# Product and composed tables loaded through GpSimd's queue, deeper buffers for the last group, longer pauses between two interleaved groups

## The chip, the cores and the metric

The kernel is one program on one core of a Trainium2 chip. The metric is device time in microseconds, the median of several executions. One profiled execution comes with it; it gives busy times, waits and a timeline of each engine. The engines are PE (TensorE, matmuls), DVE (VectorE), ACT (ScalarE), POOL (GpSimd) and SP (SyncE, which here only issues transfers, DMAs).

## What is computed

The input x is [16, 32, 128, 128] in float32. Four residual layers follow one another, each of them x = x + f(GroupNorm(x)):

- layer 0: a recurrent convolution with gates, run over the columns of a skewed image;
- layer 1: a 3x3 "adder" convolution on 8-bit values, which sums absolute differences in place of products;
- layer 2: a Hartley transform of which 32 x 32 modes are mixed between channels;
- layer 3: five edge operators, each normalised by its own mean and deviation, then a small U-net (seven 3x3 convolutions, pooling, three transposed convolutions), whose output multiplies the layer's input.

```python
# layer 1, for each of 32 outputs
out[n, f] = -sum(abs(patch(qx) - qw[f]))
# layer 2
xm = dht2d(x)[:, :, :32, :32]
z = einsum('bixy,ioxy->boxy', xm, yeven) + einsum('bixy,ioxy->boxy', flip(xm), yodd)
out = dht2d(embed(z)) / (H * W)
# layer 3
y = concat([norm(edge_k(x)) for k in range(5)]); y = conv1(y); y = maxpool2(y) ...
return x * conv7(deconv3(...))
```

## The kernel before

**Stages.** `stage0` (line 101) does layer 0 in about 870 us. `rest` (441) does layers 1 to 3. Layer 1 runs image by image in `Differences.run` (627). DVE (line 705, tile d_dve) and ACT (line 702, tile d_act) make the differences, 128 x 8192 elements in fp16 at a time, and PE adds them up by matmuls with a selection matrix (line 592). Layers 2 and 3 go in four groups of four images. As soon as the four images of a group have left layer 1, its later layers are woven between the instructions of layer 1 for the next images. That is the work of the class `Weave`: the background work is a Python generator that yields estimated durations, negative numbers as pauses, and marks for things that must be complete; `later(us, step)` puts a step off by so many estimated microseconds, and `advance` (384) puts background work into gaps of the planned schedule. `keep_order` (419) then pins the order of instructions on each engine for this whole stretch, which lasts from about 890 to 5989 us. I call it the front.

**The drain.** When layer 1 is over, the rest of the third group (number 2) and the whole of the last group (number 3) remain. `drain` (403) takes steps of the two generators in turn, always from the one that is behind, and so puts the two groups' instructions side by side; there is no pinned order there. The last group is a copy of the object `After` with pools on the other side of SBUF and an accumulator pool of its own. The drain takes from 5989 us to the end.

**One group**, in order:

1. `forward` (974): loads rows of the image (tile xh, four buffers, 992), centres them (DVE, 1014), transforms along both axes with matmuls (1061, 1076, 1031). The 32 x 32 modes come out of PSUM by a DVE copy into xm (1035, two buffers) and are stored to DRAM (1041). `modes` (1105) reads them back in another arrangement into xs and xw (1114, xw has two buffers), and DVE adds the flipped copy (1121, 1128). `weights` (1134) loads the mixing matrices, 1 MB each (tile mix, 1136, three buffers).
2. `mixing` (1139): 512 matmuls (1149), results stored to z_d. It yields pauses of 5 us at line 1159.
3. `back` (1176): reads z (1198) and the residual rows xr (1191, four buffers), transforms back (1212, 1257), adds (1235), stores x3 (1241). The images of layer 3's input go in frames of 16 rows with a margin, tile xp, a ring of two (`frames`, 1280; load 1299, normalise on ACT 1301, zeroed edges by POOL 1308).
4. `statistics` (1320): the means and deviations of the edge operators come from products of the image with shifted copies of itself (PE, 1345), multiplied with five tables gm of 210 KB each (DVE, 1405 and 1406, tile es_w). Three gm buffers are filled at line 1333, tables 3 and 4 at line 1412, once a buffer is free.
5. `first_layers` (1445): the edge operators and conv1 are composed into one set of weights wf (DVE, 1471 and 1473) from ten tables v of 720 KB each (1458, three buffers). `conv1` (1603) applies them (PE 1617, 1633, 1661), reading the frames again.
6. `small_layers` (1485) and `Composed.round` (838, matmuls 849 and 874) do the U-net's inside, `last` (1717) the last convolution, the multiplication with the layer's input (tile xr, loaded at 1731 into two buffers, each a quarter of the rows of the four images, in four DMAs; multiplied at 1752, evicted from PSUM at 1789) and the store (1768).

All these loads and stores are issued by SP, one after the other in one queue. If an issue has to wait for a buffer or for data, everything after it in the program waits behind it.

Of the kernel before, what the change touches and what calls it, by code (L numbers as in the profile page):

```python
# [19 lines left out]
M1 = 32  # L20
# [279 lines left out]
class Weave:  # L300
# [10 lines left out]
    def __init__(self, work):  # L311
        self.work, self.pending = work, None
        self.pe = self.dve = self.act = self.now = self.base = 0.0
        self.until = self.ready = 0.0
        self.draining = self.alone = False
        self.finished, self.count, self.put_off, self.for_act, self.ends = -1, 0, [], [], {}

    def later(self, us, step):
        self.count += 1
        v = self.base + us, self.count, step  # L320
        self.put_off.append(v)
        return v
# [36 lines left out]
    def step(self):  # L359

        v = self.pending or next(self.work, None)
        self.pending, wait, us = None, 0.0, 0.0
        if v is None:
            return None
        if v is SUMMED:
            wait = self.lag()
        elif isinstance(v, tuple) and v[0] == "done":
            late = v[1] in self.put_off
            self.done(v[1])
            end = self.ends[v[1][1]]  # L370
            wait = 2.0 * late if self.draining else end - self.now + 0.3
        elif isinstance(v, tuple):
            if v[1] > self.finished:
                self.pending = v
                return None
        elif v < 0:
            wait = -v
        else:
            us = v
        if wait > 0:  # L380
            self.until = self.now + wait
        return us
# [20 lines left out]
def drain(*weaves):  # L403

    live = list(weaves)
    for w in live:
        w.draining = True
    while live:
        w = min(live, key=lambda w: w.now)
        us = w.step()  # L410
        w.now = max(w.now + (us or 0.0), w.until)
        w.due(float("inf") if us is None else w.now)
        if us is None:
            live.remove(w)
            for w in live:
                w.alone = True

# [23 lines left out]
def rest(nc, tc, cst, sel16, bias, m1, r1, a, d, out):  # L441


    with ExitStack() as ctx:
# [13 lines left out]
        end.side, end.ps = "right", ctx.enter_context(tc.tile_pool(name="c_ps", bufs=4, space=PSUM))  # L458
        end.spare = bg
        end.weave = Weave(end.work([NG - 1]))  # L460
        end.weave.now = end.weave.base = weave.now
# [441 lines left out]
class After:  # L903


    def __init__(self, nc, tc, side, sm, ps, cst, bias, a, d, stat, out):
        self.nc, self.tc, self.side, self.ps, self.cst, self.bias = nc, tc, side, ps, cst, bias
        self.a, self.d, self.stat, self.out = a, d, stat, out
        self.spare, self.banks = None, 0
        store = [d["up"][i] for i in range(3)]  # L910
        self.up5 = Composed(nc, sm, a, "deconv1", "conv5", bias[:, 7:8], bias[:, 4:5], store[0])
# [62 lines left out]
    def forward(self, g):  # L974

        nc, tc, cst, d, weave = self.nc, self.tc, self.cst, self.d, self.weave
        x2, xm_d, z_d = d["x2"], d["xm"], d["z"]
        with self.pool("t_m") as mp:
            mr = mp.tile([128, 2, 4, C], F32, name="mr")
# [5 lines left out]
            with self.pool("t_t") as tp, ExitStack() as rows:  # L985
                xp = rows.enter_context(self.pool("t_x", 4))

# [6 lines left out]

                xh = [load(n) for n in range(4)]
                mv = tp.tile([128, 4, 2], F32, name="mv2")
# [29 lines left out]
                def second(n):  # L1026
# [6 lines left out]
                    def out():  # L1033
                        xm = tp.tile([128, 4, M1], F32, name="xm", bufs=2)
                        nc.vector.tensor_copy(xm.rearrange("p q k -> p (q k)"), p[:, :128])
# [44 lines left out]
                for n in range(10):  # L1080
                    if n < 7:
                        centred(n + 1)
                    if n < 8:
                        yield first(n)
                        if n + 4 < 8:
                            xh.append(load(n + 4))
                    if 1 <= n < 9:
# [8 lines left out]
                rows.close()  # L1096
                wp = rows.enter_context(self.pool("t_w", 3))
                wt = [self.weights(wp, i) for i in range(3)]
                yield -36.0
# [5 lines left out]
    def modes(self, g, b, pool, xs, steps):  # L1105

        nc, weave, xm_d = self.nc, self.weave, self.d["xm"]
        xw = pool.tile([128, 16, 32], F32, name="xw", bufs=2)
        first = xm_d.offset + (4 * g + b) * 32768
# [29 lines left out]
    def mixing(self, g, xs, wp, wt):  # L1139
# [5 lines left out]
        for ky in range(M1):  # L1145
# [12 lines left out]
            yield 1.0  # L1158
            if ky % 4 == 3 and 8 < ky < M1 - 1:
                yield -5.0  # L1160
# [15 lines left out]
    def back(self, g, load):  # L1176


        nc, tc, cst, d, weave = self.nc, self.tc, self.cst, self.d, self.weave
        x2, x3, z_d = d["x2"], d["x3"], d["z"]  # L1180

        with self.pool("t_z") as zp_, self.pool("t_r", 4) as rp:

# [12 lines left out]
            for blk in range(4):  # L1196
# [3 lines left out]
                )  # L1200
            for n in range(4):
                residual(n)
# [27 lines left out]
            def take_out(n, pf):  # L1230
# [9 lines left out]
                def store():  # L1240
                    nc.sync.dma_start(rows(n)(x3), xr[n])
                    ready[n + 4] = weave.later(6.0, lambda: reload(n + 4)) if n < 12 else None

                ready[n + 4] = weave.later(4.0, store)

# [24 lines left out]
            take_out(*previous)  # L1270
            weave.later(7.0, lambda: [load(ch, half) for ch in range(2) for half in range(2)])
            mv = zp_.tile([128, 1, 2], F32, name="mv3")
# [7 lines left out]
    def frames(self, g, pool):  # L1280
# [4 lines left out]
        nc, x3, weave = self.nc, self.d["x3"], self.weave  # L1285
        ring = [pool.tile([128, 20, W + 4], F32, name=f"xp{i}") for i in range(2)]
        for t in ring:
            nc.vector.memset(t[:, :, 0], 0.0)
            nc.vector.memset(t[:, :, W + 3], 0.0)

        def parts(ch, half):

            lo, hi = max(16 * ch - 2 + 10 * half, 0), min(16 * ch + 8 + 10 * half, H)
            off = lo - (16 * ch - 2)
            return ring[ch % 2], lo, hi, ring[ch % 2][:, off : off + hi - lo, 2 : W + 2]

# [19 lines left out]

        chunk = lambda ch: ring[ch % 2]
        return load, normalise, chunk

    def statistics(self, g, pool, frames, sides, out, tables):  # L1320
# [8 lines left out]
        load, normalise, chunk = frames  # L1329
        ready = {(n // 2, n % 2): normalise(n // 2, n % 2, 0.5 + 4.0 * n) for n in range(4)}  # L1330
        gm = [pool.tile([128, GRAM], F32, name="gm", bufs=3) for _ in range(3)]
        for k in range(3):
            nc.sync.dma_start(gm[k], self.a["gram"][:, k])
        f = pool.tile([128, 24], F32, name="es_f")
# [19 lines left out]
        for ch in range(H // 16):  # L1354
            xp = chunk(ch)
            yield ("done", ready[ch, 0])
            for l in range(2, 18):
# [28 lines left out]
                def following(ch=ch, half=half):  # L1386
                    load((ch + 2) % 8, half)
                    if ch + 2 < H // 16:
                        ready[ch + 2, half] = normalise(ch + 2, half, 18.0)

                ready[ch + 2, half] = weave.later(2.0, following)
            yield -1.0
# [9 lines left out]
        for k in range(5):  # L1402
            for blk in range(4):
# [4 lines left out]
                if blk % 2:  # L1408
                    yield -1.0
            if k < 2:  # L1410
                gm.append(pool.tile([128, GRAM], F32, name="gm", bufs=3))
                nc.sync.dma_start(gm[k + 3], self.a["gram"][:, k + 3])
        yield -2.0
# [31 lines left out]
    def first_layers(self, g, fp, frames, y2):  # L1445
# [4 lines left out]
        b1 = fp.tile([128, 4], F32, name="b1")  # L1450
        with self.pool("e_v", 3) as pool:
            v = []

            def table():

                k, half = len(v) // 2, len(v) % 2
                v.append(pool.tile([128, 45, 32], F32, name="v"))
                nc.sync.dma_start(
                    v[-1].rearrange("p t o -> p (t o)"), self.d["fold"][k, :, 1440 * half : 1440 * half + 1440]
                )  # L1460

            with self.pool("e_s") as es:
                yield from self.statistics(g, es, frames, sides, ops, lambda: [table() for _ in range(3)])
            yield -0.5
# [138 lines left out]
    def conv1(self, g, pool, frames, y1, sides, wf, b1):  # L1603
# [9 lines left out]
        load, normalise, chunk = frames  # L1613
        ready = {(n // 2, n % 2): normalise(n // 2, n % 2, 4.0 + 3.0 * n) for n in range(4)}
        p = self.acc()
# [33 lines left out]
        for ch in range(H // R):  # L1649
# [38 lines left out]
            yield SUMMED  # L1688
            if ch + 2 < H // R:
                for half in range(2):  # L1690
                    load(ch + 2, half)
                    ready[ch + 2, half] = normalise(ch + 2, half, 26.0 + 4.0 * half)
            out = []
# [23 lines left out]
    def last(self, g):  # L1717

        nc, tc, cst, weave = self.nc, self.tc, self.cst, self.weave
        with self.pool("l_y") as yp, self.pool("l_x", 2) as xp:  # L1720
            y6 = self.y6
# [11 lines left out]

            xr = [load(0), load(1)]

# [30 lines left out]
            def store(x, unit):  # L1766
                for j in range(4):
                    nc.sync.dma_start(at(self.out, unit, j), x[32 * j : 32 * j + 32])
                following[unit] = weave.later(10.0, lambda: reload(unit)) if unit < 2 else None

            def reload(unit):
                xr[unit] = load(unit + 2)
                following[unit] = None
# [5 lines left out]
            for unit in range(4):  # L1779
                complete(unit - 2)  # L1780
                x = xr[unit % 2]
                for pr in range(2):
# [186 lines left out]
```

## Time and profile before

| | before |
|---|---|
| median of 7 runs | 7224.34 us (7214.95 to 7239.58) |
| profiled execution | 7239.58 us, of which the span of the profile is 7237.6 us |
| PE busy | 5640.6 us, 78% |
| DVE busy | 5846.7 us, 81% |
| ACT busy | 5501.1 us, 76% |
| POOL busy | 52.1 us, 31 instructions |
| DMA, mean rate over the span | 100 GB/s |

The profiled execution happens to be the slowest of the seven, 15.2 us above the median. The page's second part divides the span into 40 equal slices of 181 us, with one digit for the busy tenths of each engine. From slice 6 to slice 33 DVE and ACT stand at 8 or 9, which is the front; from slice 34 on PE is the busiest. A list of waits gives for every engine the line that waited, the thing it waited for, the sum in us, the number of waits and the longest. A timeline line gives the start, the duration, engine, line and tiles, and in square brackets how long the engine had been idle and who released it.

### The profile page before, as it was taken

The page shows a single profiled execution, that of the slowest core. Times are in us where ns is not written, and L with a number is a line of the kernel's source. Part 1 is how long each engine was busy: PE and PEld are TensorE (multiplying, and loading weights), DVE is VectorE, ACT ScalarE, POOL GpSimd, SP SyncE. Part 2 cuts the span into 40 slices and gives each one's busy share as a digit, 9 for nine tenths or more (in the row PEclk, how much of TensorE's full clock was granted, in tenths as well). Part 3 has the DMA queues.
Part 4 walks back from the last instruction along what each step waited for, and adds up shares of the span by engine and source line. Part 5 has one row for each costly group of instructions (what it writes and reads, how often), then busy time and mean ns, then how long its engine had stood idle before and what let it go on. Part 6 is the DMA issues. An engine that isn't in the chain of part 4 may idle for free. (4 is left out here: it accounts for less than half of the span.)

```text
span 7237.6 us, 271421 instructions
## 1 busy us (share of the span) xinstructions
PE 5640.6 (78%) x127740; PEld 3009.0 (42%) x127740; DVE 5846.7 (81%) x7095; ACT 5501.1 (76%) x3100; POOL 52.1 (1%) x31
## 2 busy tenths in 40 slices
PE   4878567777777776999777786999776775797896
PEld 3666333333434342333334342333332443544564
DVE  7787699999989988999999998999998994234324
ACT  2555399999999988999999998999998991121222
POOL 0000000000000000000000000000000000000000
PEclk9899799999989898999888997999888997798897
DMA  8664211111132432221343343121243245352324
GB/s 312 227 203 150 78 65 57 51 58 51 43 111 83 141 101 70 63 74 44 77 123 105 111 121 96 61 66 50 64 112 99 79 128 140 95 157 83 86 59 104
DMA packets 374319, 722.57 MB, mean 100 GB/s; under 512 B 50896, under 2 KB 219856, under 8 KB 362320
## 3 DMA queue, kind: packets, MB, share of 16 engines
q1 hardware_dynamic: 372768, 704.58, 32.1%
q8 instruction: 999, 16.37, 1.0%
q14 instruction: 120, 0.98, 0.0%
q10 hardware_dynamic: 432, 0.64, 0.0%
HBM read 507.28 MB, written 164.32 MB: 93 GB/s over the span
## 5 line engine op out<-in xcount | busy, mean ns | idle before, releaser
L702 ACT ACTIVATE d_act<-q,neg 128x8192 f16<-128x8192 f16 (+1 forms) x631 | 4464.1, 7145 | 243.3 <-PE acc L592 193.6
L705 DVE TENSOR_SCALAR d_dve<-q,qw 128x8192 f16<-128x8192 f16 (+1 forms) x1673 | 3858.5, 2361 | 194.8 <-PE acc L592 152.6
L592 PE MATMUL acc<-d_dve,sel 128*32 128x512 f16 x26768 | 1868.5, 402 | 551.9 <-DVE d_dve L705 504.4
L592 PEld LDWEIGHTS <-sel 128*32 128x32 f16 x36864 | 1026.1, 100 | 2219.9 <-issue 1566.7
L1661 PE MATMUL acc<-xp,wf 32*32 32x512 f32 x25600 | 1033.1, 621 | 28.1 <-issue 22.8
L592 PE MATMUL acc<-d_act,sel 128*32 128x512 f16 x10096 | 730.1, 411 | 359.9 <-ACT d_act L702 348.9
L1661 PEld LDWEIGHTS acc<-xp,wf 32*32 32x32 f32 x25600 | 425.0, 104 | 396.0 <-issue 311.2
L622 PE MATMUL acc<-q,zero 128*32 128x512 f16 x7248 | 520.3, 399 | 0.0
L207 PE MATMUL pg<-h,wb 64*64 64x20 f32 (+15 forms) x4096 | 402.9, 323 | 96.4 <-DVE h L256 54.7
L1600 ACT ACTIVATE y<-pooled,b 32x128 f32<-32x128 f32 x488 | 195.0, 400 | 372.4 <-DVE pooled L1586 365.9
L849 PE MATMUL acc<-y,u_conv 32*32 32x256 f32 (+1 forms) x9728 | 353.3, 462 | 80.8 <-issue 51.8
L1305 ACT ACTIVATE xp<-xp,shift,stats 128x1280 f32<-128x1280 f32 (+1 forms) x128 | 182.9, 1434 | 277.2 <-DMA xp<-x_d 264.0
L244 ACT ACTIVATE gt<-pg,bias 128x20 f32<-128x20 f32 (+15 forms) x1024 | 315.7, 375 | 77.5 <-PE pg L207 70.7
L207 PE MATMUL pg<-e,wb 64*64 64x20 f32 (+15 forms) x4096 | 358.8, 319 | 16.9 <-DVE e L260 4.5
L207 PEld LDWEIGHTS pg<-h,wb 64*64 64x64 f32 x4096 | 249.9, 156 | 132.7 <-DVE h L256 82.4
L622 PEld LDWEIGHTS <-zero 128*32 128x32 f16 x7248 | 218.0, 101 | 201.0 <-issue 43.0
L207 PE MATMUL pg<-xn,wb 64*64 64x28 f32 (+61 forms) x4096 | 287.0, 305 | 9.6 <-ACT gt L244 3.0
L207 PEld LDWEIGHTS pg<-e,wb 64*64 64x64 f32 x4096 | 254.4, 157 | 95.6 <-DVE e L260 67.4
L1345 PE MATMUL acc<-xp 32*64 32x204 f32 (+3 forms) x8576 | 243.1, 343 | 35.8 <-ACT xp L1311 25.7
L255 ACT ACTIVATE th<-c 128x20 f32<-128x20 f32 (+15 forms) x256 | 81.3, 320 | 238.7 <-DVE c L253 237.3
L849 PEld LDWEIGHTS acc<-y,u_conv 32*32 32x32 f32 x9728 | 171.1, 110 | 190.5 <-issue 126.7
L1789 DVE TENSOR_SCALAR s<-acc,l_ms,l_one 128x512 f32<-128x512 f32 x128 | 101.9, 821 | 164.6 <-PE acc L849 164.6
(212 smaller groups left out, 4263.9 us busy)
## 6 DMA issues: line engine op xcount, KB each, us to landing
xr<-x_d SPq DMA_DIRECT2D x192, 512.0 KB
xp<-x_d SPq DMA_DIRECT2D x112, 640.0 KB
q<-q_d SPq DMA_DIRECT2D x32, 2145.0 KB
x_d<-xr SPq DMA_DIRECT2D x128, 512.0 KB
x_in<-in_x_dram SPq DMA_DIRECT2D x16, 2048.0 KB
res<-in_x_dram SPq DMA_DIRECT2D x64, 512.0 KB
xn<-in_xs_dram SPq DMA_DIRECT2D x64, 512.0 KB
xn<-xn SPq DMA_DIRECT2D x128, 256.0 KB
```

The source lines that it names most:

```text
L207: nc.tensor.matmul(bank[c][q][64 * pair : 64 * pair + 64, :, :width], wb[half, 4 * kind + KIND[q]].rearrange("p b o -> p (b o)"), v[half], ...
L244: nc.scalar.activation(gt[:, q, :, :n], bank[c][q][:, :, :n], AF.Tanh if q == G else AF.Sigmoid, bias=bias[:, KIND[q] : KIND[q] + 1],)
L592: self.nc.tensor.matmul(acc[k][32 * j : 32 * j + 32, :], self.sel16[:, i // 9, :], d[:, row : row + 4, c : c + W], start=first, stop=last,)
L622: self.nc.tensor.matmul(acc[k][32 * j : 32 * j + 32, :], self.zero, q[:, :4, :W], start=False, stop=False)
L702: nc.scalar.activation(dst, src, AF.Relu, bias=self.neg[:, i : i + 1])
L705: nc.vector.tensor_scalar(dst, src, self.qw[:, i : i + 1], 0.0, ALU.subtract, ALU.max)
L849: nc.tensor.matmul(acc[blk][32 * j : 32 * j + 32, o : o + rows * n], t[part, 4 * par + tap, :], src[part, top : top + rows, left : left + ...
L1305: nc.scalar.activation(v, v, AF.Identity, bias=self.shift3, scale=self.stats3[:, 1])
L1345: nc.tensor.matmul(gram[blk][j : j + width, at : at + n], xp[part, l, 2 + j : 2 + j + width], xp[part, rows, j : j + width + 4], start=sta ...
L1600: nc.scalar.activation(d, s, AF.Identity, bias=bj)
L1661: nc.tensor.matmul(acc[blk][32 * j : 32 * j + 32, :], tap_of("all", tap)[rows], xp[rows, 4 * j + kh : 4 * j + kh + 4, kw : kw + W], start= ...
L1789: nc.vector.tensor_scalar(s.rearrange("p r w b -> p b r w"), acc[blk].rearrange("p (b r w) -> p b r w", b=2, w=64), istd[:, blk : blk + 1] ...
```

## The change

1. The loads of the tables gm (lines 1333 and 1412) and v (1458) are issued by GpSimd instead of SP: 15 loads for each group, 60 in all.
2. Buffer numbers are taken from a dictionary. In the front xm gets three buffers instead of two; the other numbers stay (xh 4, xw 2, mix 3, xr 4, frames 2, gm 3, v 3, xr of the last layer 2). For the last group, which runs in the drain, all are raised: xh 8, xm 8, xw 4, mix 6, xr 8, frames 4, gm 5, v 6, xr of the last layer 4. Loads ahead and conditions for reloads follow these numbers.
3. While two groups are drained side by side, pauses and `later` times are multiplied by 1.5; when one is left, by 1.
4. The pauses of 5 us in `mixing` are left out while draining.

```diff
     def later(self, us, step):
-        v = self.base + us, self.count, step
+        v = self.base + us * self.stretch, self.count, step
...
         elif v < 0:
-            wait = -v
+            wait = -v * self.stretch
...
     for w in live:
-        w.draining = True
+        w.draining, w.stretch = True, 1.5
...
             for w in live:
-                w.alone = True
+                w.alone, w.stretch = True, 1.0
...
+        end.buffers = {"t_x": 8, "xm": 8, "xw": 4, "t_w": 6, "t_r": 8, "frames": 4, "gm": 5, "e_v": 6, "l_x": 4}
         end.weave = Weave(end.work([NG - 1]))
...
+        self.buffers = {"t_x": 4, "xm": 3, "xw": 2, "t_w": 3, "t_r": 4, "frames": 2, "gm": 3, "e_v": 3, "l_x": 2}
...
-                        xm = tp.tile([128, 4, M1], F32, name="xm", bufs=2)
+                        xm = tp.tile([128, 4, M1], F32, name="xm", bufs=self.buffers["xm"])
...
-            if ky % 4 == 3 and 8 < ky < M1 - 1:
+            if ky % 4 == 3 and 8 < ky < M1 - 1 and not weave.draining:
                 yield -5.0
...
-        gm = [pool.tile([128, GRAM], F32, name="gm", bufs=3) for _ in range(3)]
-        for k in range(3):
-            nc.sync.dma_start(gm[k], self.a["gram"][:, k])
+        gm = [pool.tile([128, GRAM], F32, name="gm", bufs=tables_ahead) for _ in range(tables_ahead)]
+        for k in range(tables_ahead):
+            nc.gpsimd.dma_start(gm[k], self.a["gram"][:, k])
...
-                nc.sync.dma_start(gm[k + 3], self.a["gram"][:, k + 3])
+                nc.gpsimd.dma_start(gm[-1], self.a["gram"][:, len(gm) - 1])
...
-        with self.pool("e_v", 3) as pool:
+        with self.pool("e_v", self.buffers["e_v"]) as pool:
...
-                nc.sync.dma_start(
+                nc.gpsimd.dma_start(
                     v[-1].rearrange("p t o -> p (t o)"), self.d["fold"][k, :, 1440 * half : 1440 * half + 1440]
                 )
...
-        with self.pool("l_y") as yp, self.pool("l_x", 2) as xp:
+        with self.pool("l_y") as yp, self.pool("l_x", self.buffers["l_x"]) as xp:
...
-            xr = [load(0), load(1)]
+            xr = [load(unit) for unit in range(ahead)]
```

## The prediction

> **What bounds the kernel now.** I read the page's first and second parts, then the waits of DVE and ACT in the front, then the timelines around the longest of them, then the drain by windows. The page first:
>
> ```profile
> PE 5640.6 (78%) x127740; PEld 3009.0 (42%) x127740; DVE 5846.7 (81%) x7095; ACT 5501.1 (76%) x3100; POOL 52.1 (1%) x31
> DVE  7787699999989988999999998999998994234324
> ACT  2555399999999988999999998999998991121222
> ```
>
> The shares of the whole span mislead. From slice 6 to 33 (890 to 5989 us) DVE and ACT are both full; a hole there in both engines is lost time, and work on POOL or SP costs nothing while it is off their path. From slice 34 on neither is full, and PE carries the drain. The waits of DVE in the front:
>
> ```profile
> DVE d_dve L705 <- PE acc L592: 152.6, 94, 14.6
> DVE es_w L1405 <- DMA gm<-in_gram_dram: 40.3, 2, 24.6
> ...
> DVE xm L1035 <- DMA xm_d<-xm: 34.6, 3, 25.0
> DVE xw L1121 <- DMA xw<-xm_d: 13.7, 4, 5.3
> DVE wf L1473 <- DMA v<-fold_d: 10.9, 4, 7.2
> ```
>
> Three of them hang on tables or buffers that the change touches. The first hole for gm, on SP's queue, DVE and ACT:
>
> ```profile
> 2711.07 0.33 SPq L1412 DMA_DIRECT2D gm<-in_gram_dram  x1
> 2711.44 0.55 SPq L559 DMA_DIRECT2D q<-q_d  x1
> 2718.22 0.33 SPq L1412 DMA_DIRECT2D gm<-in_gram_dram  x1
> ```
>
> ```profile
> 2755.60 0.60 DVE L1405 TENSOR_TENSOR es_w<-acc,gm 128x420 f32<-128x420 f32 x1 [24.60 <-DMA gm<-in_gram_dram]
> ```
>
> ```profile
> 2767.13 14.14 ACT L702 ACTIVATE d_act<-q,neg 128x8192 f16<-128x8192 f16 x2 [17.02 <-PE acc L592]
> 2783.49 7.13 ACT L702 ACTIVATE d_act<-q,neg 128x8192 f16<-128x8192 f16 x1 [2.23 <-PE acc L592]
> ```
>
> The last table was issued in time (2718) but came at 2755, behind the 2145 KB load of q that SP had issued just before. DVE stood 24.6 us, and ACT 17.0 + 2.2 soon after, since PE's accumulators came late. The second hole (4410) is DVE 15.7, ACT 11.4 + 1.8. The drain (PE busy by windows: 112 of 240 us from 6000, then 344 of 360, 132 of 180, 231 of 260, 132 of 197) is open at its start, in its middle and at its end. At the end:
>
> ```profile
> 7187.45 1.41 DVE L1752 SCALAR_TENSOR_TENSOR xr<-xr,l_ms,s 128x512 f32<-128x512 f32 x2 [11.78 <-DMA out_dram<-xr]
> 7212.73 1.42 DVE L1752 SCALAR_TENSOR_TENSOR xr<-xr,l_ms,s 128x512 f32<-128x512 f32 x2 [10.38 <-DMA out_dram<-xr]
> ```
>
> Two buffers of xr are reloaded only after the store before has left; both waits lie on the last stretch.
>
> **What the Trainium skill says.** (1) "DMA: Bandwidth & Descriptors", section "Queues, rings and completion order": each DMA engine goes round between the queues that have work, and takes one queue's in order. So gm on a queue of its own need not sit behind q. The trace agrees with the order within one queue (37 us for a table of 210 KB behind q); sharing between queues no run here shows yet. (2) Same page, "Issuing engines are not separate DMA queues": all end on the same 16 engines; another issuer saves only issue time. That holds for bandwidth; here the gain is order. (3) "SBUF — State Buffer", "Who interferes with whom": VectorE in its fast two-port mode and GpSimd exclude each other for a whole instruction, and a transfer issued by GpSimd waits to write its descriptors until VectorE lets go. The trace agrees for instructions:
>
> ```profile
> 3718.71 6.99 POOL L983 MEMSET xs<- 64x2048 f32 x1 [495.92 <-PE acc L849]
> ...
> 6005.73 1.80 POOL L983 MEMSET xs<- 64x2048 f32 x1 [306.13 <-DMA x_d<-xr]
> ```
>
> 1.80 us in the drain, where no L705 runs; up to 6.99 in the front beside it. DVE pays as well: six d_dve beside the two memsets at 1562 took 16.98 us where 6 x 2.27 = 13.6 is usual, so 3.4 for two memsets; four at 5388 took 10.80 instead of 9.2, so 1.6. For transfers no row of before shows it.
>
> **The change part by part**, in us on the end, minus is gain.
>
> *gm on GpSimd's queue.* The two holes go: DVE 24.6 + 15.7 = 40.3, ACT 19.2 + 13.2 = 32.4. Both engines must gain for the front to gain, so I take ACT's: -32. DVE's further 8 become waits for PE. What is late next is PE's sum for the following unit, which is inside the usual 152.6 of small waits.
>
> *v on GpSimd's queue.* DVE's waits for v (10.9 in 4) came where SP stood in other issues; half go on both engines: -5 (0 to -11). SP stands 122.3 us behind "SPq L1458 <- DVE wf L1471", a wait for a v buffer, with the loads of xq, xr and xp queued behind. ACT's waits for those sum to 25.0 + 24.9 in the front, but the long ones (22.9 at 2505, 17.4 once at the start) lie away from a v wait, so nothing more. On GpSimd, v 4 to 10 wait for wf, and only memsets of xp edges stand behind: nothing, as they are needed tens of us later.
>
> *gm beside xp.* At 2505 ACT waits 22.9 for xp loads that now share the engines with gm, where they went ahead: +3 (0 to +8).
>
> *Loads written by GpSimd while L705 runs.* 15 loads for each of two groups and the first three of the third: 33 in the front. Bounds for one: nothing, if descriptors fall into DVE's gaps (below nothing is excluded, as writing them speeds nothing up); 1.7 us of DVE, as half the 3.4 of two memsets, each 1.8 us long. I take 0.4, a quarter, since a load of 128 rows gives less to write than 64 x 2048 elements: 33 x 0.4 = +13 (0 to +56).
>
> *xm with three buffers.* The wait of 25.0 at 5536 was for a store issued at 5528.84, behind q of 5520.58. With a third buffer this copy waits for the store of 5520.12, ahead of q, so it passes. But the reload into xw (SP 5561.70, straight after) needs the later store, and DVE meets it some four d_dve (9.2 us) on: the hole moves. -2 (0 to -10).
>
> Front: -32 - 5 + 3 + 13 - 2 = -23.
>
> *Start of the drain (6000 to 6240).* PE has 128 us idle here. Its 512 matmuls of mixing (35 us) began at 6152.87 after 30.5 for xs, as DVE waited 50.7 in all for xw in eight waits. Eight xm and four xw shorten these. But SP now has eight xh loads of 1 MB where four stood ahead of the seven xp loads for group 2's statistics; one lands 4 to 7 us after the last, so 4 x 5 = 20 later for the statistics. And the reloads into the third and fourth xw stand in the new order behind six mix loads (the old one had four at 6160.90, 11.85 us of issuing): I put mixing 16 later. Against that, v is no longer issued between the z stores (13 us at 6191.52), and PE's 24.9 for wf gets shorter, 15 on each. +20 + 16 - 15 - 15 = +6 (-25 to +25; the two sides overlap, hence the width). The long PE stretch behind, 344 of 360 busy, hides what the 1.5-fold pauses and the missing pauses of mixing move: 0.
>
> *Middle (6600 to 6780).* 40 instructions es_w and their reductions, 1.25 us a pair, put 20 pairs ahead of DVE's pooled, for which PE waits 16.8. Six v and five gm in advance and longer pauses put them a little elsewhere: -4 (+4 to -12).
>
> *End.* Four buffers hold all four quarters, so the 11.8 + 10.4 = 22.2 go. The next thing is PE's rounds of 8 to 10 us for each half quarter; part of the wait hid them (PSUM holds a few). I count three quarters: -16 (-11 to -21). xr x16 ahead of the stores takes SP's issue time from no one.
>
> Drain: +6 - 4 - 16 = -14. **Sum: -37**, so 7239.6 becomes 7202.6 in the profiled execution. That execution is 15.2 above the median, so I take the sum off the median: 7224.3 - 37 = 7187.
>
> **Rivals.** *The drain opens* (7150): at its start the xw waits and the 30.5 of PE all go, the xp loads keep up, so -30 in place of +6. For: DMA share there is 0.53, not full. Against: SP's one queue orders it, and the new order puts mix ahead of the reloads.
>
> *Waits move* (7212): xm's hole sits at L1121, v comes just late, the start of the drain loses 12, and what stays is 7224.3 - 8 - 4 = about 7212, with front -8 (gm's 32 less 24 of moved waits) and drain +12 - 16 = -4. For: PE's accumulators are waited for 94 times as it is. Against: the two holes for gm have one plain cause each.
>
> *GpSimd is shut out* (7262): each load keeps DVE 1.7 us and comes 1.0 later in wf, 2.7 x 33 = +89 instead of +13: -37 + 76 = +39 on the median, slower. For: the memset of 6.99 and L705 back to back for 5000 us. Against: memsets of xp edges took 1.4 to 4.6 there and no more. It decides from (13 + 37) / 33 = 1.5 us a load.
>
> That the change doesn't do what it says I exclude: the compiled order has the loads on POOL's queue, and DVE, ACT and PE in the front unchanged.
>
> **How the numbers follow.** Likeliest 7187, 0.48, own range 7165 to 7205; drain opens 0.14; waits move 0.20; shut out 0.18. What a measurement can tell from no change is 0.2%, 14 us, so faster is below 7210, slower above 7239. Faster: 0.47 + 0.14 + 0.08 = 0.69. Same: 0.01 + 0.12 + 0.02 = 0.15. Slower: 0.16. For the range, the port's bounds alone give 7187 - 13 = 7174 and 7187 + 43 = 7230; with the start of the drain at its ends (31 below, 19 above) 7143 and 7249. I take 7140 to 7248; left out are a third of the second case (0.05) and two thirds of the last (0.12).
>
> **What would show it.** Right: the waits for gm gone from DVE's list, ACT busy through 2755 and 4410; no wait for out_dram at L1752; mean L705 within 1% of 2361 ns (33 x 0.4 over 1673 is 8 ns). Wrong: L705's mean 20 ns or more up, or wf waiting for v ten times and more, is the port; a wait of 25 us at L1121 near 5545 is the moved hole; mixing before 6140 is the open drain. An xp wait of ACT above 30 us would say that the queues compete.

## The result and the profile after

The changed kernel takes 7207.32 us (median of 14 runs, 7198.93 to 7216.87), the kernel before 7222.32 on the same chips (36 runs). The ratio is 0.9978 with a 95% interval of 0.9971 to 0.9985: faster, by 15 us, where 37 were forecast. The profiled execution took 7203.82 us, with a span of 7200.6. Against the profiled execution of before the span is 37 us shorter, but that one was the slowest of its seven: that this equals the forecast is chance, and spans are not compared below without the medians.

The first page lines of after, and its transfer queues:

```profile
PE 5615.3 (78%) x127740; PEld 2992.6 (42%) x127740; DVE 5844.4 (81%) x7099; ACT 5498.3 (76%) x3100; POOL 114.3 (2%) x91
DVE  7787689999998989999999999999998994234223
q0 software_dynamic: 7040, 33.80, 1.4%
```

POOL has 60 instructions more, the 60 loads, and 33.8 MB go through a queue of their own. Of DVE's 8s in the front those of slices 16 and 25 have become 9s, where the two holes for gm were; that of slice 31, where xm waited, is still there. Slices 34 to 40, the drain, look much as before. The waits of DVE in the front, the answer to the five lines shown before:

```profile
DVE d_dve L708 <- PE acc L595: 153.8, 92, 18.1
DVE xw L1126 <- DMA xw<-xm_d: 46.0, 7, 12.4
...
DVE sides L1384 <- ACT xp L1319: 5.7, 3, 2.7
```

The waits for gm (40.3) and v (10.9) are gone. The wait of xm for its store (34.6) is gone too, but xw, which reads what was stored, went from 13.7 to 46.0: the sum of the two, 48.3 before, hardly moved. The copies into sides, which wait for the frames, stand at 5.7 as before (5.3). The front as a whole is read from the first and last start of DVE's difference line (before, then after):

```profile
L705 DVE TENSOR_SCALAR d_dve<-q,qw x1673: 2289/2349/3975, 918.5 to 5984.5; 128x8192 f16<-128x8192 f16 x123, 128x8320 f16<-128x8320 f16 x63
```

```profile
L708 DVE TENSOR_SCALAR d_dve<-q,qw x1673: 2289/2350/4006, 920.9 to 5932.8; 128x8192 f16<-128x8192 f16 x123, 128x8320 f16<-128x8320 f16 x63
```

5066.0 us before, 5011.9 after: the front gained more than the whole kernel. (One trace gives such a length to some 9 us: e2 below, whose front is that of before, took 5057.5, where 5 or less was expected between the two.) The median of one instruction is 2349 and 2350 ns and the mean 2361 in both. The 30 differences that ran beside a load of GpSimd took 70.86 us in all, the same 30 before 70.91, so these loads cost DVE nothing that shows. The drain lost: from the last difference to the last instruction of an engine, which the last transfer follows by 12 us, 1238.7 us before and 1253.6 after. Cut at the ends of the two long conv1 stretches (windows of both traces, up to the last transfer): start 249 to 262 us, first conv1 342 to 330, middle 133 to 140, second conv1 334 to 333, tail 192 to 200.

### The profile page after: what moved, and what is told of

The parts are those of the page before. It is cut to its first block, busy times and chain, and to the rows that moved or that the text cites. A ratio compares the mean times of both kernels' runs of the same rounds, so it can differ in the third digit from the quotient of the medians.

```text
span 7200.6 us, 271424 instructions
## 1 busy us (share of the span) xinstructions
PE 5615.3 (78%) x127740; PEld 2992.6 (42%) x127740; DVE 5844.4 (81%) x7099; ACT 5498.3 (76%) x3100; POOL 114.3 (2%) x91
## 5 line engine op out<-in xcount | busy, mean ns | idle before, releaser
L708 DVE TENSOR_SCALAR d_dve<-q,qw 128x8192 f16<-128x8192 f16 (+1 forms) x1673 | 3858.5, 2361 | 197.5 <-PE acc L595 153.8
```

Of the source, the lines that this page charges most:

```text
L708: nc.vector.tensor_scalar(dst, src, self.qw[:, i : i + 1], 0.0, ALU.subtract, ALU.max)
```

## The experiments

All numbers in us. "d" is the median less that of before on the same chip, with the interval of the ratio.

| run | d | ratio |
|---|---|---|
| the change | -15 | 0.9978 [0.9971, 0.9985] |
| e1_front_only | -33 | 0.9955 [0.9942, 0.9969] |
| e2_drain_only | +15 | 1.0025 [1.0015, 1.0035] |
| e3_no_stretch | -3 | 0.9993 [0.9985, 1.0001] |
| e4_two_xr | -13 | 0.9985 [0.9978, 0.9992] |
| e5_change_again | -13 | 0.9980 [0.9974, 0.9987] |
| e6_buffers_of_before | -33 | 0.9960 [0.9946, 0.9973] |
| e7_four_xh | -25 | 0.9962 [0.9948, 0.9976] |
| e8_two_frames | -3 | 0.9997 [0.9987, 1.0006] |
| e9_front_four_xr | -34 | 0.9953 [0.9940, 0.9966] |
| e10_xr_loaded_twice | -15 | 0.9981 [0.9972, 0.9989] |
| e11_only_frames | -46 | 0.9934 [0.9922, 0.9947] |
| e12_xh_and_xr_back | -34 | 0.9951 [0.9938, 0.9964] |
| e13_gm_alone | -27 | 0.9958 [0.9945, 0.9970] |
| e14_loads_in_halves | -23 | 0.9967 [0.9955, 0.9980] |
| e15_mix_xm_xw | -36 | 0.9953 [0.9940, 0.9967] |

Single ratios are good to some 0.13%, or 9 us; smaller differences are read from the traces or left open. My theory after this profile was that the front had gained more than the whole and that the drain gave part of it back; the rival was my recorded sum, with gains in both.

**Front alone and drain alone.**

```diff
# e1
-        end.buffers = {"t_x": 8, "xm": 8, "xw": 4, "t_w": 6, "t_r": 8, "frames": 4, "gm": 5, "e_v": 6, "l_x": 4}
+        end.buffers = {"t_x": 4, "xm": 2, "xw": 2, "t_w": 3, "t_r": 4, "frames": 2, "gm": 3, "e_v": 3, "l_x": 2}
-        w.draining, w.stretch = True, 1.5
+        w.draining, w.stretch = True, 1.0
-            if ky % 4 == 3 and 8 < ky < M1 - 1 and not weave.draining:
+            if ky % 4 == 3 and 8 < ky < M1 - 1:
# e2: end.buffers, stretch and pauses as in the change; "xm" of the front 2; and
-            nc.gpsimd.dma_start(gm[k], self.a["gram"][:, k])
+            nc.sync.dma_start(gm[k], self.a["gram"][:, k])
# the same for the other gm load and for v
```

> Tables gm and v on GpSimd's queue and three xm buffers as in the change; the last group has the buffer numbers of before, pauses are not stretched and mixing keeps its pauses. Theory (the front gained more than the whole change, and the drain gave part of it back): the last L705-line difference ends 35 to 52 us earlier than before, the drain is as long as before (1251 us from there to the end, +-6), and the time is 30 to 50 below before, so faster than the whole change. Rival (the recorded sum: front -23, drain -14): 20 to 25 below before, slower than the change with all its parts by some 14.

> Tables stay on SP's queue and xm has two buffers in the front; the deeper buffers of the last group, the stretched pauses and the missing pauses of mixing are as in the change. Theory (the drain gave back): front as before within 5 us, drain 1260 to 1270 us instead of 1251, so 8 to 20 us slower than before. Rival (the recorded sum): the drain is 14 shorter, so 14 us faster than before.

Measured -33 and +15. e2's interval excludes the gain of 14 of the recorded sum; e1's, 22 to 42, reaches down to the forecast's 23. The two add up to -18, the change to -15. So the theory holds in its main part: the front alone is worth twice the change, and the drain's part of the edit makes the kernel slower. (Up to the last instruction of an engine e1's drain took 1218 us, where the 1239 of before, within 6, was expected; later runs with that drain, e13 and e14, took 1235 and 1234. So one execution's drain is good to some 20 us, and e2's 1249 alone would not have settled it; the medians do.)

**Longer pauses.** e3: `w.stretch = 1.0`, buffers deep. e6: the buffers of before, pauses long.

> The change with the factor 1.0 in place of 1.5; all else as in the change. Theory A (the longer pauses put the two groups' work in a worse order): the drain comes back to 1250 us or less, 10 to 15 below the changed kernel. Theory B (the deeper buffers' loads fill SP's queue ahead of what is needed, the pauses matter little): within 5 us of the changed kernel.

> The change, but the last group has the buffer numbers of before; longer pauses and mixing without pauses stay. Theory A (the deeper buffers cost the drain): close to the front-only kernel, 10 to 18 below the changed kernel. Theory B (the longer pauses and the missing pauses cost it): within 5 of the changed kernel.

By ratio e3 came out 0.0015 (11 us) above the change, against both of its theories. But the chips differ, the two intervals meet at 0.9985, and the drain in e3's trace (1255) is no longer than in the change's two (1254, and 1259 in e5), so that the longer pauses help with deep buffers is suggested and not shown. e6 came out with the front-only kernel (0.9960 and 0.9955), so with the old buffers they change nothing that can be measured. The loss of the drain belongs to the deeper buffers, theory A of e6.

**Which buffers.** e5 is the change itself on the chip of e6 to e8; e7 has `"t_x": 4`, e8 `"frames": 2`, e4 `"l_x": 2`, e12 `"t_x": 4` and `"l_x": 2`, all else as in the change; e15 is e11 (at the end of this section) with `"t_w": 6`, `"xm": 8` and `"xw": 4`.

> The changed kernel as it is, for the same chip as the next three. Both theories: 12 to 20 below before. Its profile tells how far two profiled executions of one kernel differ: drain within 10 us of 1254.

> The change with four xh in the last group instead of eight, so that four loads of 1 MB no longer stand ahead of seven loads of frames in SP's queue. Recorded step (four loads ahead cost the statistics 20 us): 8 to 15 below the changed kernel, and PE's wait before L743, 24.9, falls to some 12. Rival (that wait comes from the order of DVE's copies into sides, which this leaves): within 4 of the changed kernel and the wait stays.

> The change with two frames instead of four in the last group. Theory (frames ahead delay the loads and the products of group 3, whose es_w ends at 668 us of the drain instead of 646 in the front-only kernel): 5 to 12 below the changed kernel, es_w ends before 655. Rival (frames ahead help, SP's later loads are not needed earlier): 3 to 10 above it.

e7: 12 below the change on its chip. PE's waits at the start of the drain, of the change and then of e7:

```profile
PE acc L1424 <- DVE es_red L1415: 26.9, 1, 26.9
PE acc L743 <- DVE ns_v L740: 24.9, 1, 24.9
PE acc L1081 <- DVE ta L1070: 22.0, 2, 12.2
```

```profile
PE acc L1424 <- DVE es_red L1415: 27.1, 1, 27.1
...
PE acc L743 <- DVE ns_v L740: 10.0, 1, 10.0
```

With four xh the wait before L743 falls from 24.9 to 10.0, and conv1 of group 2 starts at 250 us of the drain instead of 263 (e5). DVE's order, with its copies into sides ahead of ns_v, is the same in both, so it is the loads: four more xh of 1 MB stand ahead of frames in SP's queue (the change issues them at 5966.88 and the seven frames at 5979.61, e7 the seven at 5971.39), the frames come late, ACT and DVE behind them, then PE. The other wait, 27 for es_red, is one of order: PE's sums of the statistics now stand ahead of mixing, and stay there in e7. It is no loss by itself, for without it PE waits 33 for xs at this place (e6, e11).

e8: 10 above the change on its chip. Four frames are a gain, the rival's side; es_w ends at 670 in both.

> The change with two buffers instead of four for the xr of the last layer of the last group. Theory (PE's own pace sets the tail: in the changed trace the waits of DVE for out_dram are gone and its waits for PE at the eviction grew from 164.6 to 200.0): within 4 us of the changed kernel, the two waits of 10 to 12 us come back. Rival (the recorded sum: four buffers are worth 16): 11 to 21 us slower than the changed kernel. Third (loading 8 MB at once slows the start of the tail): 5 us faster.

> The change with four xh and two xr in the last group, the other buffers deep. If the two costs add (13 for xh, 0 to 8 for xr): 15 to 20 below the changed kernel, level with the front-only kernel, 30 to 35 below before. If only xh counts: as the run with four xh, 27 below before.

> The kernel with only frames deep, and mix 6, xm 8 and xw 4 as in the change too. If these cost the drain (six loads of 1 MB ahead of the reloads in SP's queue): 8 to 15 above the kernel with only frames deep, the matmuls of mixing begin 10 us or more later than its 174 us of the drain. If they are neutral: within 5, and the rest lies in xr of back, gm and v.

e4 is on another chip than any run of the change; by ratio it is 0.0007 (5 us) above it, inside the intervals, so the medians show no gain from going back to two xr. Its trace has a shorter end: 105.8 us from l_ms to the end, the change 113.2 and 111.4 in its two profiles. e12 was to be level with the front-only kernel and is (0.9951). It is 12 above e11 on the same chip, with intervals that overlap, though both have four frames, four xh and two xr; so one of the other deep buffers may cost too. e15 is 0.0019 (14 us) above e11 by ratio, as if mix, xm and xw were that cost, but its trace shows mixing begin at 173 us of the drain (174 in e11) and a drain of 1224.8 (1230.7). Neither theory is settled by that. What xr of `back`, gm and v cost in the drain was not tried alone.

**The tail.** e9 is e1 with `"l_x": 4`. e10 adds to e9:

```diff
+            if self.side == "right":
+                dp = extra.enter_context(self.pool("l_d", 4))
+                for unit in range(4):
+                    again = dp.tile([128, 4, 8 * W], F32, name="again")
+                    for j in range(4):
+                        nc.sync.dma_start(again[32 * j : 32 * j + 32], at(self.d["x3"], unit, j))
```

> The front-only kernel with four buffers instead of two for the xr of the last layer of the last group. Recorded sum: 16 (11 to 21) below the front-only kernel, the stretch from l_ms to the end 91 to 96 us instead of 107. Theory (PE's rounds set the tail, and PE stands while the loads are in flight): no gain, the stretch 107 to 114 us, time 0 to 8 above the front-only kernel.

> As the run before it, and after the 16 loads of xr another 16 of the same rows into tiles that nothing reads: 8 MB more in flight at the start of the tail, no new wait for any engine but SP. Theory (PE stands some 5 us at a time for its instructions while loads are in flight): PE has two to four more gaps of about 5 us with no releaser, the tail is 8 to 20 longer. Rival (PE's gaps are its order and its dependencies, whatever the traffic): within 4 us of the run before.

e9 took 0.9953, e1 0.9955, and the stretch from l_ms to the end 106.8 and 107.2: four buffers are worth nothing, where 16 were forecast. Where the 16 went is in DVE's waits in the tail, of e1 and then of e9, which differ in this number alone:

```profile
DVE s L1800 <- PE acc L852: 37.4, 7, 14.9
DVE xr L1763 <- DMA xr<-x_d: 22.7, 2, 11.9
```

```profile
DVE s L1800 <- PE acc L852: 59.9, 8, 15.1
```

The same in before and the change, from 7070 us on:

```profile
DVE s L1789 <- PE acc L849: 38.3, 7, 14.9
DVE xr L1752 <- DMA out_dram<-xr: 22.2, 2, 11.8
```

```profile
DVE s L1800 <- PE acc L852: 66.3, 8, 15.0
```

60.1 in two lines and 59.9 in one; 60.5 in two lines before, 66.3 in one line after. The waits for a buffer lay beside PE's own time; with them gone DVE waits for PE as long. From l_ms on PE waits for nothing that the profile names in any of the four; its idle time without a releaser is 33 us in e1, 34 in e9, 33 before and 38 in the change. Three such gaps of the change, while the 16 loads of xr (issued from 7065 to 7090) are in flight:

```profile
7089.02 0.28 PE L877 MATMUL acc<-bias,u_conv 32*32 32x4 f32 x11 [4.90 <-issue]
7098.53 0.70 PE L852 MATMUL acc<-y,u_conv 32*32 32x256 f32 x10 [5.59 <-issue]
7107.48 1.84 PE L852 MATMUL acc<-y,u_conv 32*32 32x256 f32 x42 [4.75 <-issue]
```

The second and third stand at their places, 23 and 32 us after l_ms, in all eight traces with four xr and in none of the nine with two, where other gaps come later. With four xr this stretch takes 110.5 to 114.4 us in six traces with other deep buffers, 106.8 in e9 and 110.7 in e10; with two it takes 105.8 to 110.0.

e10 shows such gaps under more traffic, in a place that I had not meant: the scheduler put the extra loads ahead, into conv1 of group 3. SP's timeline and PE's, of e10:

```profile
6915.82 0.78 SPq L1751 DMA_DIRECT2D again<-x_d  x2
6916.70 1.11 SPq L1307 DMA_DIRECT2D xp<-x_d  x2
6917.86 28.70 SPq L1751 DMA_DIRECT2D again<-x_d  x14
```

```profile
6926.99 6.07 PE L1671 MATMUL acc<-xp,wf 32*32 32x512 f32 x128 [3.98 <-issue]
...
6954.68 5.96 PE L1671 MATMUL acc<-xp,wf 32*32 32x512 f32 x128 [3.25 <-issue]
6962.82 4.49 PE L1671 MATMUL acc<-xp,wf 32*32 32x512 f32 x128 [2.19 <-issue]
```

Five gaps (two are left out here), 14.7 us, once every 128 matmuls, in a stretch of conv1 that runs through without the extra loads (e9). conv1 took 358 us instead of 332, and the time rose by 0.0028 (20 us). The gaps are over half of that; the matmuls between them were slower as well, at a granted clock of 0.80 from 6926 to 6968 us (1.00 just before and after). The tail proper rose by 4 only, so the forecast was right in size and wrong in place.

**The front's two terms.** e13 is e1 with v on SP's queue. e14 is e1 with each table load cut in two:

```diff
-            nc.gpsimd.dma_start(gm[k], self.a["gram"][:, k])
+            for h in (slice(0, GRAM // 2), slice(GRAM // 2, GRAM)):
+                nc.gpsimd.dma_start(gm[k][:, h], self.a["gram"][:, k, h])
# the same for the other gm load and for v
```

> The front-only kernel with v back on SP's queue, so gm alone goes through GpSimd. Theory (gm is worth what DVE stood, some 38 to 40, v some 8 to 9, less 12 for frames that come later): 5 to 10 above the front-only kernel, waits of wf for v of some 10 back, 25 to 28 below before. Rival (the recorded sum: gm 32, v 5): the same order of sizes, 3 to 6 above. Third (v's queue is what matters, as SP stood 122 us behind waits for a v buffer): 20 or more above the front-only kernel.

> The front-only kernel with every load of gm and v issued as two of half the width: 60 more transfers from GpSimd, 33 of them in the front, the same bytes. Recorded term (0.4 us of DVE for each): 13 above the front-only kernel, L708's mean 8 ns up. Upper bound of the term (1.7 each): 56 above. Theory (GpSimd waits for DVE, and DVE not for GpSimd): within 5, L708's mean 2361 to 2366 ns, waits of wf for v may appear as GpSimd takes 2 us for each.

e13: the waits of wf for v are back (11.1 in 4), and DVE falls 8.8 us behind e1 around the last of them (4430 us), 6 over the whole front. By time it is level with e1 within the intervals. e14: by time it is 10 above e1, nearer the recorded 13 than the theory's 5, but inside the intervals of the two. The traces decide. DVE's mean is 2361 ns with twice as many loads (2365 in e1, and in e2 without any), where 8 ns more were forecast; the 44 differences that ran beside a load took 103.82 us, the same ones before 103.87. The front is 4 longer than e1's (5021.2 against 5017.3 from the first start to the last). So GpSimd's loads do not hold DVE. DVE holds them, shown by POOL's timeline of the change:

```profile
2712.55 0.54 POOL L1421 DMA_DIRECT2D gm<-in_gram_dram  x1 [39.20 <-DVE es_w L1414]
2719.70 0.54 POOL L1421 DMA_DIRECT2D gm<-in_gram_dram  x1 [6.61 <-DVE es_w L1414]
2752.34 2.12 POOL L1467 DMA_DIRECT2D v<-fold_d  x1 [32.10 <-DVE wf L1480]
```

0.54 us beside es_w, 2.12 beside a difference. Of 36 loads in the front (the recorded sum counted 33) 24 took 2.0 to 2.5 us, each of them beside a difference; in the drain, where there are no differences, one takes 0.5. And what stands behind them on POOL waits: at 4208 us ACT had to wait for the memset of a frame's edge, queued behind the gm loads.

```profile
4208.56 0.21 ACT L1319 COPY xp<-xp 128x10 f32<-128x10 f32 x1 [4.77 <-POOL xp L1316]
```

In e1 the same wait was 7.0, and in e14, with six loads ahead of the memset, 12.3; there DVE falls 3.8 us behind e1, about what e14's front is longer.

**The best version.** e11 is e6 with `"frames": 4`.

> The change with the buffer numbers of before for the last group, except four frames; longer pauses stay. If four frames are worth alone what they were beside the other buffers (12): 10 to 15 below the kernel with all buffers of before, some 40 below before, the best so far. If they paid only there, where more is loaded ahead: within 5 of it.

0.9934, 46 below before on its chip and 0.0026 (19 us) below e6, 14 by the medians: frames are worth at least as much alone as beside the others, and this kernel is faster than the change by 0.0044, some 32 us, clear of both intervals.

## Why the prediction was wrong

The direction was right; the size, -37 against -15, was not, and the time lies inside the range. The direction came from the front alone, which gave more than forecast; the drain, forecast at -14, cost 15 (e2), and the step that failed there is the last one, *End*. Among the rivals "waits move" came nearest in time (7212), but not in place: in the front most of the waits went, and the drain is what lost.

- *gm, -32.* The mechanism held. The size was low: by the starts of the same DVE instruction, e2 against e1, the front gains 23.8 at the first hole and 13.9 at the second, 38 in all, which is the whole of DVE's wait for gm in e2 (37.7). Counting ACT's pieces next to the hole left out those that PE passed on: at the first hole ACT has gained 19.7 after 50 us, the forecast's 19.2, and 24.1 after 80.
- *v, -5.* About right: 8.8 at the last waits in e13's trace, 6 over its front.
- *gm beside xp, +3, and "only memsets of xp edges stand behind: nothing".* The first fell: ACT's wait for xp transfers in the front is 23.0 in e2 and 23.5 in e1. The second fell the other way: the memset behind the gm loads on POOL held ACT 4.8 to 7.0, and e1 loses 6.7 of its lead there (4240 to 4340 us). Another 4.5 is lost at 3938 us, in e1 and not in the change; no run explains it.
- *GpSimd's writing, +13.* Fell: nothing on DVE, in the change and in e14. The two memsets that I had priced it from hold DVE (three differences beside such memsets took 3.97 to 4.01 us in the change too), these loads do not. The Trainium skill's page "SBUF — State Buffer", "Who interferes with whom", says that VectorE and GpSimd block each other for a whole instruction, and that the one that issues first goes first. For these loads the trace shows one direction only, GpSimd waiting (0.54 and 2.12); the other I had taken from the memsets.
- *xm, -2.* Right, with its mechanism: at 5487 us 28 to 29 are gained on e2, and 23 to 26 are lost again within the next 60, on waits for xw (12.4, 7.0, 7.9, 3.9).
- *Front, -23.* 40 from the first to the last difference, e2 against e1 (5057.5 and 5017.3), 33 by the median of e1. By the trace: gm 38, v 8, xm 5, less the 7 behind the memset and the 4.5, so 40. What the forecast missed is above all the 13 of GpSimd's writing and 6 of gm.
- *Start of the drain, +6.* The four xh loads cost 13 with everything behind them (e7), where the step said 20, and the offsets of 15 and 15 did not come: mixing began 24 later, 14 of them by the xh loads (e5 and e7), and the wait for wf shrank from 24.9 to 13.1 only. The wait for es_red is not why mixing is late, for e15 has it too (26.7) and begins mixing at 173 us, before at 166. +13.
- *Middle, -4.* First conv1 and middle together 475 before, 470 after; about right, and it is the four frames that give it (e8, e11).
- *End, -16.* This is the step that failed: "The next thing is PE's rounds of 8 to 10 us for each half quarter; part of the wait hid them (PSUM holds a few). I count three quarters." Nothing of it was to be had, neither 16 nor the 11 of its lower bound: the waits of 22.2 turned into waits for PE, whose rounds and gaps set the tail. Alone, four buffers give 0 (e9). In the change the end is 8 longer than before; against e4, with two xr beside the other deep buffers, the tail is longer by 6 to 7 in the traces. That cost is not shown, for e4's median is no better than the change's, and it is not separated from PE's granted clock in that stretch (0.79 in e4, 0.77 and 0.73 in the two of the change).

With -33 for the front and +13, -5, -1 and +8 for the drain the sum is -18; the median says -15.

## What to carry to other kernels

A small table that is needed soon belongs on a queue where no large transfer stands ahead of it: here the new order, with some 5 of it from a third xm buffer, was worth 33 us. A wait that an engine shows beside the engine that it feeds from is worth only what is left once the other's own pace is counted: list all waits of the consumer over the stretch, and see whether their sum can fall. Deeper buffers are not free when one queue issues for all: an extra load ahead can delay what is needed first (four xh cost 12 us here, two more frames gained 10 to 19), so deepen one buffer at a time.

## What the runs showed of the hardware

The loading of PE's instructions seems to be one of the things that PE waits for. In the trace's packets the queue called "instruction" brings 16 KB at a time. The page of the change has 17.35 MB of instructions for 271424 of them, 64 bytes each, so one packet holds 256 instructions, or 128 matmuls with their weight loads (an estimate from these two numbers). The five gaps of e10 come every 128 matmuls, and each gap shown above, in the tail too, ends 2.5 to 3.1 us after such a packet starts. While the extra loads of e10 are in flight (DMA share 0.98 from 6926 to 6968 us) these packets come 9.0 us apart, and right after that (0.02) 3.8. The Trainium skill, "Runtime: NRT & Kernel Launch", "Instruction fetch mechanics", gives the 16 KiB blocks and calls the cost of crossing one mostly hidden; here PE stood 2.2 to 5.6 us at a time while 8 MB were on their way, and 8 MB more cost 20 us of the whole. That the late packet is what PE waits for is read from this coincidence, and no run took it apart from other effects of the traffic.
